# A two-layer graph convolution on one Trainium2 core: the order of its preparation, its PSUM banks and the row targets are rearranged

## The chip, the cores and the metric

The kernel runs on one core of a Trainium2 chip. The metric is the device time of one execution in microseconds. A core has five engines with an instruction queue each: PE (TensorE: matmuls and transposes), DVE (VectorE), ACT (ScalarE), POOL (GpSimd) and SP (SyncE, which only issues transfers). PE writes to PSUM, from where DVE or ACT copy the values to the on-chip memory. The engines wait for each other through semaphores.

## What is computed

The graph has N = 6250 nodes with 128 features each and E = 106250 edges, sorted by their target node. An edge has 64 message features and a time; the 32 cosines of the time difference to its source node are put ahead of the message. Two convolutions follow each other, and the sum with x is normalised:

```python
def _transformer_conv(h, edge_attr, src, dst, Wq, bq, Wk, bk, Wv, bv, We, Ws, bs):
    q = (h @ Wq + bq).reshape(n, H, C)                  # H = 2 heads of C = 64
    k = (h @ Wk + bk).reshape(n, H, C)
    v = (h @ Wv + bv).reshape(n, H, C)
    e = (edge_attr @ We).reshape(-1, H, C)
    kj = k[src] + e
    alpha = jnp.einsum('ehc,ehc->eh', q[dst], kj) / jnp.sqrt(C)
    a = <softmax of alpha over the edges of one target>
    out = segment_sum((v[src] + e) * a[:, :, None], dst, n)
    return out.reshape(n, H * C) + h @ Ws + bs

rel_t_enc = jnp.cos((last_update[src] - t)[:, None] * time_w + time_b)
edge_attr = jnp.concatenate([rel_t_enc, msg], axis=-1)
h = _transformer_conv(x, edge_attr, src, dst, ...)       # weights 1
h = relu((h - mean(h)) / sqrt(var(h) + 1e-5) * bn_g + bn_b)
h = _transformer_conv(h, edge_attr, src, dst, ...)       # weights 2
out = layernorm(x + h)
```

## The kernel before

The edges are cut into 104 chunks of 1024 (eight tiles of 128 edges, one edge per partition), and the nodes so that a chunk belongs to a window of 64 target nodes. Instead of keys and values per edge, the weights are multiplied together beforehand, and a table per target node (`tables`, L629) holds what its edges' raw features are multiplied with; a chunk's scores are then matmuls of its transposed rows with the table of its window.

**The rows of the source nodes** come by indirect transfers on POOL: one gather of 128 rows per tile, eight per chunk. In the first convolution they read `xv_d`, a copy of x with the node's time beside each row (L900), in the second h. The gathers write to a ring of seven slots in on-chip memory. Those of chunks 0 and 1 are made before `xv_d` exists: they read x (L1610), and their times are picked out of a table of hours by matmuls (`pick_times`, L670). A gather is issued four rounds ahead of its use. From chunk 7 on, when a slot is used again, it is tied to instructions of PE: the first gather of chunk k + 4, issued in round k, to the last matmul of round k − 1's sums (L1063).

**Rounds.** Round k of a convolution (L1150 and after) has the scores of chunk k (L1016), the divisions of chunk k − 2 (`divide`, L1072 to L1096), the lowest score per edge (L1024, DVE), the exponentials (L1031, ACT), the transposes of chunk k + 1 (L973, L985), the encoding of a later chunk's times (L938 to L946 on DVE, the sine L952 on ACT) and the sums of chunk k − 1 (L1063). At one place in a round, work from outside of the chunks is pulled (`rest`, L1389): in the first rounds two pieces each, at first the row targets (`targets`, L762), which say to which target row a chunk's boundary belongs, and then the tables of the other nodes, 512 nodes at a time. The order of a round's instructions on each engine is as written.

**The preparation** (`tile_gnn_resnorm`, L1484) comes ahead of both convolutions. Its steps are written as generators, each of which stops after one piece, and `step` calls put the pieces in an order. They are: the loads; columns of sources, targets and times from rows (`columns`, L1592 and after, transposes of PE and copies of DVE); the first gathers (L1610); the boundaries of the windows by a scan (L1646); the plan check, which gathers doubts about the input in `edge` and sets `oki` (L1696); the copy `xv_d` (`pass_features`, L526); the transposed x (`turn_features`, L650: four transposes of PE into PSUM, one copy of ACT, thirteen times); the products of the weights (`matrices`, L580); the picked times; and the tables of the first 512 nodes. When it is through, each engine reads `oki` (L1723) and branches to `ordered` (L712), which holds the convolutions, or to a general program that is not run here. POOL's next instructions after the branch are the gathers from chunk 2 on.

**PSUM in the preparation.** Four kinds of buffers: `fpt`, three tiles that are cut into twelve slices of 128 columns, each used once (`bank`, for weight products and codes); `fpx`, two buffers (`wide`, for columns, x0 and tables); `ftm`, two (`aside`, for the picked times and the boundaries); and `fxp`, a single one, for the transposes of x (`turning`).

**Queues.** Transfers are issued by SP and ACT (and the indirect ones by POOL). ACT's queue starts with rows of sources and targets, the weights of the first convolution (L1541), the column bs1 (L556) and two small pieces of the target rows, the tail (L1545); behind these stands ACT's first copy (L660).

Of the kernel before, what the change touches and what calls it, by code (L numbers as in the profile page):

```python
# [7 lines left out]
F32 = mybir.dt.float32  # L8
# [60 lines left out]
SQRT = 3  # L69
SWITCH = NC - 3  # L70
# [440 lines left out]
def load_features(nc, pl, x, node_vec):  # L511
# [6 lines left out]
    nc.sync.dma_start(pl.times, node_vec[:NF * P].rearrange("(p b) -> p b", b=NF))  # L518
    for i, (b0, b1) in enumerate(pl.cuts):
        nc.sync.dma_start(rows[:, b0:b1, 1:], x[:NF * P, :].rearrange("(p b) d -> p b d", b=NF)[:, b0:b1])  # L520
        if i == 0:
            nc.sync.dma_start(pl.rest[:NR, 1:], x[NF * P:N, :])
            nc.sync.dma_start(pl.rest[:NR, 0:1], node_vec[NF * P:N].rearrange("(p a) -> p a", a=1))

# [150 lines left out]
def pick_times(nc, pl, pool, bank, srows, node_vec):  # L675
# [16 lines left out]
    for k in range(EARLY):  # L692
        times = split_rows(pl, k)[2]
        for u in range(T // 4):
            pb = bank()
            nc.tensor.matmul(pb[:NA], one[:, k], hi[:, u * GE:(u + 1) * GE], start=True, stop=True)
            oh = pool.tile([NA, GE], F32, name="foh", bufs=2)
            nc.vector.tensor_scalar(oh, pb[:NA], lane[:NA], None, op0=OP.is_equal)
            yield
            pc = bank().rearrange("p (i n) -> p i n", n=P)  # L700
            for i in range(4):
                nc.tensor.matmul(pc[:, i], oh[:, i * P:(i + 1) * P], pl.hours, start=True, stop=True)
            for i in range(4):
                t = u * 4 + i
                junk = pool.tile([P, P], F32, name="fjunk", bufs=2)
                nc.vector.scalar_tensor_tensor(junk, pl.place_of, lo[:, t, k:k + 1], pc[:, i], op0=OP.is_equal,
                                               op1=OP.mult, accum_out=times[:, t, 0:1])
            yield
# [3 lines left out]
def ordered(ctx: ExitStack, tc: tile.TileContext, pl, x, dst, edge_attr_64, conv2, bn_g, bn_b, out):  # L712
# [49 lines left out]
    def targets():  # L762
# [11 lines left out]
        for i in range(NQ):  # L774
            nc.vector.tensor_sub(away[:, 0, i], nbq[:, :, i], nbq[:, :, 0])
# [4 lines left out]
        for q in range(NQ):  # L780
            nc.vector.tensor_sub(away[:, 2, q], past[:, NQ - 1], past[:, q])
# [29 lines left out]
    def conv(c, extra, first_blocks=None):  # L811
# [339 lines left out]
        with cs, tc.manual_schedule():  # L1151
            if c == 0:
                nc.vector.tensor_copy(rate, tw)
                nc.vector.tensor_copy(phase, tb)
            ended = None
# [179 lines left out]
    with tc.tile_pool(name="fpw", bufs=2) as pw:  # L1335
# [52 lines left out]
        def rest():  # L1388
# [5 lines left out]
            yield from targets()  # L1394
            yield
            for b0 in range(1, NT):
                yield from tables(nc, pl, 0, xT[:, b0 * GE:(b0 + 1) * GE], b0, pw, lambda: pl.bank())
# [93 lines left out]
def tile_gnn_resnorm(ctx: ExitStack, tc: tile.TileContext, x, src, dst, edge_attr_64, edge_weight, node_vec,  # L1491
# [11 lines left out]
    with tc.tile_pool(name="plan", bufs=1) as pl, tc.tile_pool(name="planw", bufs=2) as mw, \  # L1503
# [33 lines left out]
        nc.sync.dma_start(got.hours[:N // P], node_vec[:N // P * P].rearrange("(a b) -> a b", b=P))  # L1537
        nc.sync.dma_start(got.hours[N // P:, :N % P], node_vec[N // P * P:].rearrange("(a b) -> a b", a=1))
# [3 lines left out]
        got.bs1 = load_column(nc.scalar, keep, "fbs1", conv1["bs"])  # L1542
# [32 lines left out]
        def bank():  # L1575
            return next(fresh)
# [183 lines left out]
```

## Time and profile before

| | us |
|---|---|
| median of 3 runs (2184.24 to 2189.97) | 2184.45 |
| profiled execution | 2188.76 |
| its span | 2187.0 |
| PE busy (share of the span) | 1667.6 (76%) |
| POOL busy | 1578.8 (72%) |
| DVE busy | 1113.2 (51%) |
| ACT busy | 979.0 (45%) |

The mean granted clock of PE is 0.878 of full speed. A row of the time line has the start, the duration, the engine, the line of the kernel, the operation, output and input tiles (numbers of buffers left out), how many instructions it stands for, and in brackets the idle time of that engine before it and what released it. PEld is the weight load of PE, "ACTq" and the like are an engine's issuing of transfers. A releaser is worked out from semaphore events: the one that came last by the profile. Where an engine first loads `oki` and branches, as POOL does ahead of its first gather from `xv_d`, the branch itself is not shown.

### The profile page before, as it was taken

How to read it: one execution, taken by the hardware profiler on the slowest of the kernel's cores; microseconds unless marked ns; L12 is line 12 of the kernel's file. 1: busy time of each engine (PE TensorE's matmuls, PEld its weight loads, DVE VectorE, ACT ScalarE, POOL GpSimd, SP SyncE). 2: the span in 40 equal slices, each digit the busy share in tenths (PEclk: the TensorE clock that was granted, in tenths of full speed). 3: DMA queues.
4: the chain of work that ended last, by engine and by line, in shares of the span. 5: the costliest groups of instructions: out<-in, count | busy, mean ns of one | idle time of the engine just before them, and what ended most of it. 6: DMA issues, size and time to landing. Idle time of an engine off the chain costs nothing.

```text
span 2187.0 us, 45360 instructions
## 1 busy us (share of the span) xinstructions
PE 1667.6 (76%) x13293; PEld 981.9 (45%) x13293; DVE 1113.2 (51%) x3740; ACT 979.0 (45%) x1837; POOL 1578.8 (72%) x1686
## 2 busy tenths in 40 slices
PE   5798778767877787787767877777777877877776
PEld 3455455545454455455534433433444433443333
DVE  3676766656665766676737432333333332332233
ACT  2477666655544555576642333333332333232222
POOL 4567777777777777777637777777777777777774
PEclk9699999988988998999888887888988898888888
DMA  6578777776776777778758666676666667677662
GB/s 186 139 217 228 225 219 216 214 211 168 215 211 199 221 212 204 215 216 218 196 159 253 184 180 185 185 198 182 185 191 184 186 189 194 179 193 186 173 159 77
DMA packets 426908, 423.82 MB, mean 194 GB/s; under 512 B 297322, under 2 KB 344324, under 8 KB 423324
## 3 DMA queue, kind: packets, MB, share of 16 engines
q1 hardware_dynamic: 353344, 273.20, 43.8%
q0 software_dynamic: 53184, 109.44, 21.2%
q10 hardware_dynamic: 20124, 38.19, 4.8%
q8 instruction: 109, 1.79, 0.4%
q14 instruction: 147, 1.20, 0.2%
HBM read 274.75 MB, written 142.54 MB: 191 GB/s over the span
## 4 chain that ended last, share of the span: by engine, by line
PE 36%; DMA 33%; DVE 13%; issue 8%; POOL 4%; ACT 3%; SPq 1%; DVEq 0%; ACTq 0%; POOLq 0%
DMA fring<-hn_d,fsrcs 18%; PE fpa L1063 9%; DMA fring<-xv_d,fsrcs 8%; PE fps L1016 8%; PE fpx L973 5%; POOL fring L900 4%; PE fpg L634 3%; DMA et_d<-fet 3%; DVE farg L945 3%; PE fpe L985 2%; PE fpa L1094 2%; PE fppt L1040 1%; DVE fa L1075 1%; ACT L1031 1%; DVE farg L939 1%
## 5 line engine op out<-in xcount | busy, mean ns | idle before, releaser
L900 POOL DMA_INDIRECT fring<-xv_d,fsrcs x815 | 770.4, 945 | 287.5 <-issue 108.2
L900 POOL DMA_INDIRECT fring<-hn_d,fsrcs x775 | 734.5, 948 | 236.2 <-issue 106.7
L973 PE MATMUL fpx<-fident,fring 128*128 128x128 f32 x1664 | 326.9, 306 | 232.1 <-DMA fring<-hn_d,fsrcs 208.8
L1063 PE MATMUL fpa<-fring,fpt 128*32 128x256 f32 (+1 forms) x4128 | 407.7, 448 | 0.0
L977 ACT COPY fft<-fpx 128x512 f32<-128x512 f32 x402 | 233.5, 581 | 342.0 <-PE fpx L973 339.3
L973 PEld LDWEIGHTS fpx<-fident,fring 128*128 128x128 f32 x1664 | 223.8, 153 | 294.1 <-DMA fring<-hn_d,fsrcs 247.2
L1016 PE MATMUL fps<-fft,ftab 128*32 128x384 f32 (+1 forms) x1774 | 267.3, 526 | 69.5 <-ACT fs L1031 62.7
L1041 ACT COPY fpt<-fppt 128x384 f32<-128x384 f32 x208 | 100.0, 481 | 488.7 <-PE fppt L1040 462.6
L1063 PEld LDWEIGHTS fpa<-fring,fpt 128*32 128x32 f32 (+1 forms) x4128 | 141.6, 128 | 267.5 <-issue 175.9
L1144 DVE TENSOR_SCALAR fout<-fres,fmean,fvar 64x128 f32<-64x128 f32 x104 | 37.8, 364 | 339.9 <-ACT fvar L1142 328.0
L1094 PE MATMUL fpa<-fsel,fa 128*128 128x128 f32 x404 | 86.2, 297 | 142.3 <-DVE fsel L1079 134.0
L1024 DVE TENSOR_REDUCE flow<-fps 128x1 f32<-128x384 f32 x207 | 114.9, 555 | 111.0 <-PE fps L1016 109.8
L986 ACT COPY fet<-fpe 112x512 f32<-112x512 f32 x207 | 123.1, 595 | 83.8 <-DMA et_d<-fet 60.0
L985 PE MATMUL fpe<-fident,fring 128*112 128x128 f32 x832 | 145.3, 304 | 5.5 <-ACT fring L952 5.5
L1016 PE MATMUL fps<-fet,ftab 112*32 112x384 f32 (+2 forms) x960 | 145.5, 470 | 0.0
L1016 PEld LDWEIGHTS fps<-fft,ftab 128*32 128x32 f32 x1774 | 85.2, 118 | 133.4 <-ACT fs L1031 81.7
L945 DVE SCALAR_TENSOR_TENSOR farg<-fangles,farg 128x256 f32<-128x256 f32 x312 | 132.3, 424 | 10.7
L938 DVE TENSOR_TENSOR frel<-fring,few 128x8 f32<-128x8 f32 x104 | 18.2, 175 | 216.0 <-DMA fring<-xv_d,fsrcs 215.1
L1040 PE MATMUL fppt<-fident,fs 128*128 128x128 f32 x626 | 111.2, 287 | 18.2 <-DVE fhr L1354 7.4
L1031 ACT ACTIVATE fs<-fps,fm 128x384 f32<-128x384 f32 x207 | 120.5, 582 | 8.9 <-DVE fm L1026 7.9
L1094 PEld LDWEIGHTS fpa<-fsel,fa 128*128 128x128 f32 x404 | 48.7, 147 | 159.7 <-DVE fsel L1079 151.1
L1016 PE MATMUL fps<-fxT,ftab 112*32 112x384 f32 (+2 forms) x900 | 119.4, 497 | 1.1 <-DMA fxT<-et_d 1.1
(278 smaller groups left out, 2501.1 us busy)
## 6 DMA issues: line engine op xcount, KB each, us to landing
ea_d<-fring SPq DMA_DIRECT2D x104, 448.0 KB
et_d<-fet SPq DMA_DIRECT2D x104, 448.0 KB
fring<-ea_d SPq DMA_DIRECT2D x104, 448.0 KB
fxT<-et_d SPq DMA_DIRECT2D x104, 448.0 KB
tab_d<-fo ACTq DMA_DIRECT2D x26, 1024.0 KB
ftab<-tab_d SPq DMA_DIRECT2D x832, 32.0 KB
fring<-in_edge_attr SPq DMA_DIRECT2D x103, 256.0 KB
fring<-xv_d,fsrcs POOLq DMA_INDIRECT x815
```

Of the source, the lines that this page charges most:

```text
L900: row = nc.gpsimd.indirect_dma_start(out=f[:, t, :D + 1 - c], out_offset=None, in_=(h_d[:N, :] if k < RAW else hn_d) if c else pl.xv_d, in ...
L945: nc.vector.scalar_tensor_tensor(arg, turn, -part, arg, op0=OP.mult, op1=OP.add)
L973: last = nc.tensor.transpose(px[:, t * P:(t + 1) * P], s.x[:, u * 4 + t, 1 - c:1 - c + D], ident)
L977: nc.scalar.copy(s.ft[:, u * GE:(u + 1) * GE], px)
L985: last = nc.tensor.transpose(pe[:EC, t * P:(t + 1) * P], s.e[:, u * 4 + t], ident)
L986: copy(s.et[:, u * GE:(u + 1) * GE], pe[:EC])
L1016: steps.append(nc.tensor.matmul(s.ps[r, to:to + n], s.tab[:kd, r, i], (ets if i else fts)[:kd, at:at + n], start=i == 0, stop=i == 1 and t ...
L1024: nc.vector.tensor_reduce(low, s.ps, AX.X, OP.min)
L1031: nc.scalar.activation(s.s[:, :s.ps.shape[1]], s.ps, AF.Exp, bias=s.bias, scale=-1.0)
L1040: last = nc.tensor.transpose(pp[:, t * P:(t + 1) * P], s.s[:, t * P:(t + 1) * P], ident)
L1063: steps.append(nc.tensor.matmul(s.pa[g * GH:(g + of) * GH].rearrange("p (a d) -> p a d", a=2), s.pt[:, (g * n + t) * GH:(g * n + t + of) * ...
L1094: step = nc.tensor.transpose(s.po[:, i], s.a[:, r], s.sel[:, 0])
```

## The change

**PSUM.** The preparation has two kinds of buffers: `fpx`, four banks in turn for all its steps, `bank` being a slice of the next one; and `ftm`, four for the picked times. The single `fxp` and the one-time slices are gone.

**Picked times.** `pick_times` is cut differently. Its pieces are, chunk by chunk: `place` (two matmuls that spread a row of indices over the partitions), `find` (two comparisons), `pick` (eight matmuls); and at last `keep` for both chunks (DVE). Before, a piece was place and find, or pick and keep, of half a chunk.

**Order.** The `step` calls are placed anew. The first chunk's places, finds and picks stand ahead of the boundaries, the second's pick, the products of the weights from the keys' on, and x0 stand behind the plan check.

**Queues.** The hours go from SP to ACT, ahead of the weights; the column bs1 from ACT to SP, behind the times of the edges; the two tails from ACT to POOL, ahead of the iota for the identity; the times beside x go behind the first cut of x. On ACT a one-element copy (`warm`) stands behind the last issue.

**First convolution.** ACT loads the table of the sine by an instruction of its own at the start. The row targets' two loops of four subtractions are one subtraction each, and `targets` is pulled in two parts: the first in round 0, as before, the second in round 1 behind the first piece of the next table.

```diff
@@ load_features
-    nc.sync.dma_start(pl.times, node_vec[:NF * P]...)
     for i, (b0, b1) in enumerate(pl.cuts):
         nc.sync.dma_start(rows[:, b0:b1, 1:], ...)
         if i == 0:
...
+            nc.sync.dma_start(pl.times, node_vec[:NF * P]...)
@@ pick_times
+    def place(k):
+        for u in halves:
+            spread[u] = bank()
+            nc.tensor.matmul(spread[u][:NA], one[:, k], hi[:, u * GE:(u + 1) * GE], start=True, stop=True)
...
+    for act, k in ((place, 0), (find, 0), (pick, 0), (place, 1), (find, 1), (pick, 1), (keep, 0), (keep, 1)):
+        act(k)
+        yield
@@ targets
-        for i in range(NQ):
-            nc.vector.tensor_sub(away[:, 0, i], nbq[:, :, i], nbq[:, :, 0])
+        nc.vector.tensor_sub(away[:, 0], nbq.rearrange("a c i -> a i c"), nbq[:, None, :, 0].to_broadcast([1, NQ, NC]))
...
-        for q in range(NQ):
-            nc.vector.tensor_sub(away[:, 2, q], past[:, NQ - 1], past[:, q])
+        nc.vector.tensor_sub(away[:, 2], past[:, NQ - 1:].to_broadcast([1, NQ, NC]), past)
@@ conv
             if c == 0:
...
+                nc.scalar.add_instruction(mybir.InstLoadActFuncSet(..., act_func_set_id=TRIG))
@@ rest
-            yield from targets()
+            place = targets()
+            next(place)
             yield
             for b0 in range(1, NT):
-                yield from tables(nc, pl, 0, ..., b0, pw, lambda: pl.bank())
+                for i, _ in enumerate(tables(nc, pl, 0, ..., b0, pw, lambda: pl.bank())):
+                    yield
+                    if b0 == 1 and i == 0:
+                        next(place, None)
+                        yield
@@ tile_gnn_resnorm
-        nc.sync.dma_start(got.hours[:N // P], ...)
-        nc.sync.dma_start(got.hours[N // P:, :N % P], ...)
+        nc.scalar.dma_start(got.hours[:N // P], ...)
+        nc.scalar.dma_start(got.hours[N // P:, :N % P], ...)
...
-        got.bs1 = load_column(nc.scalar, keep, "fbs1", conv1["bs"])
+        warm = pl.tile([1, 2], F32, name="warm")
+        nc.gpsimd.memset(warm, 0.0)
+        nc.scalar.copy(warm[:, 0:1], warm[:, 1:2])
         tail = pl.tile([1, 2, NQ], I32, name="tail")
         for i, at in enumerate((-3 * P - 1, P)):
-            nc.scalar.dma_start(tail[:, i, :NQ - i], ...)
+            nc.gpsimd.dma_start(tail[:, i, :NQ - i], ...)
...
         rows(nc.sync, erows, edge_weight, CE)
+        got.bs1 = load_column(nc.sync, keep, "fbs1", conv1["bs"])
...
+        def wide():
+            return pp.tile([P, GE], F32, name="fpx", bufs=4)
         def bank():
-            return next(fresh)
-        def wide():
-            return pp.tile([P, GE], F32, name="fpx")
+            return wide()[:, :P]
         def aside():
-            return pp.tile([P, GE], F32, name="ftm")
-        def turning():
-            return pp.tile([P, GE], F32, name="fxp", bufs=1)
+            return pp.tile([P, GE], F32, name="ftm", bufs=4)
```

PE's queue in the preparation, before (L659 are the transposes of x, L696 the places, L702 the picks, L585 the transposes of weights, L600 and L604 their products):

```order
L659 MATMUL fxp<-fident,fhT 128x128 x8
L696 MATMUL ftm<-fhif,fone 49x512
L659 MATMUL fxp<-fident,fhT 128x128 x4
L585 MATMUL fpt_162<-fident,fwq_107 128x128
L585 MATMUL fpt_162<-fident,fwk_108 128x128
L702 MATMUL ftm<-fhours,foh 128x128 x4
L659 MATMUL fxp<-fident,fhT 128x128 x8
L696 MATMUL ftm<-fhif,fone 49x512
L585 MATMUL fpt_162<-fident,fwe_109 128x128
L659 MATMUL fxp<-fident,fhT 128x128 x4
L600 MATMUL fpt_163<-ftr_286,ftr_283 128x128
L604 MATMUL fpt_163<-fbq_111,ftr_286 128x1
```

And after (L660, L699, L710, L586, L601 and L605 are the same steps, L1703 is the plan check's matmul):

```order
L710 MATMUL ftm<-fhours,foh 128x128 x8
L660 MATMUL fpx<-fident,fhT 128x128 x4
L699 MATMUL ftm<-fhif,fone 49x512 x2
L660 MATMUL fpx<-fident,fhT 128x128 x8
L586 MATMUL fpx<-fident,fwq_107 128x128
L586 MATMUL fpx<-fident,fwk_108 128x128
L660 MATMUL fpx<-fident,fhT 128x128 x4
L1703 MATMUL fpx<-pones,worst 1x1
L586 MATMUL fpx<-fident,fwe_109 128x128
L660 MATMUL fpx<-fident,fhT 128x128 x4
L601 MATMUL fpx<-ftr_307,ftr_303 128x128
L605 MATMUL fpx<-fbq_111,ftr_307 128x1
```

All of them now take the next of the four banks `fpx`, the picks apart; the first chunk's picks have moved ahead of the first transposes of x, and the plan check's matmul ahead of the products of the weights.

DVE's queue in the first rounds, before, from the row targets' second part to the lowest score of chunk 1 (L1024):

```order
L788 TENSOR_SCALAR ftarget<-fpg,fhr 128x104
L792 SCALAR_TENSOR_TENSOR fhr<-fhr,ftarget 128x3
L793 SCALAR_TENSOR_TENSOR fhr<-fpg,fhr 128x3
L795 TENSOR_SCALAR fclosing<-fhr 128x2 x2
L796 TENSOR_SCALAR fhr<-fpg,fhr 128x104
L797 TENSOR_TENSOR fhr<-fhr,ftarget 128x104
L798 TENSOR_TENSOR fhr<-fhr 128x104
L799 TENSOR_TENSOR ftarget<-ftarget,fhr 128x104
L888 TENSOR_TENSOR fbits<-fdsts,fbitm 128x64
L890 TENSOR_SCALAR fring<-fbits 128x8x8
L891 TENSOR_SCALAR fring<-fbits 128x8x8
L1024 TENSOR_REDUCE flow<-fps 128x1
```

And after, from the lowest score of chunk 1 (now L1037) on (L951 to L959 are the encoding, L800 and after the targets' second part):

```order
L1037 TENSOR_REDUCE flow<-fps 128x1
L1039 TENSOR_SCALAR fm<-flow 128x1
L951 TENSOR_TENSOR frel<-fring,few 128x8
L952 TENSOR_TENSOR farg<-frel,fangles 128x256
L953 TENSOR_TENSOR farg<-farg,fangles 128x256
L955 TENSOR_SCALAR fangles<-farg 128x256
L956 TENSOR_SCALAR fangles<-fangles 128x256
L958 SCALAR_TENSOR_TENSOR farg<-fangles,farg 128x256 x3
L959 TENSOR_SCALAR farg<-farg 128x256
L800 TENSOR_SCALAR fhr<-fpg,fhr 128x104
L801 TENSOR_SCALAR ftarget<-fpg,fhr 128x104
L805 SCALAR_TENSOR_TENSOR fhr<-fhr,ftarget 128x3
```

The targets' second part has moved from ahead of that score to behind the encoding that follows it. On PE the scores of chunk 1 stood behind the target matmuls:

```order
L985 MATMUL fpe<-fident,fring 112x128 x4
L786 MATMUL fpg<-faway,pones 32x104 x12
L790 MATMUL fpg<-nbf,pones 128x3
L1016 MATMUL fps<-fft,ftab 32x384 x2
L1016 MATMUL fps<-fet,ftab 32x384 x2
```

After, these matmuls (L799, L803) come a round later, and a piece of the next table (L635) stands ahead of the scores (L1029):

```order
L998 MATMUL fpe<-fident,fring 112x128 x4
L635 MATMUL fpg<-fxT,fm_365 128x512
L1029 MATMUL fps<-fft,ftab 32x384 x2
L1029 MATMUL fps<-fet,ftab 32x384 x2
L1029 MATMUL fps<-fft,ftab 32x384 x2
L1029 MATMUL fps<-fet,ftab 32x384 x2
L1053 MATMUL fppt<-fident,fs 128x128 x3
L986 MATMUL fpx<-fident,fring 128x128 x4
L998 MATMUL fpe<-fident,fring 112x128 x4
L986 MATMUL fpx<-fident,fring 128x128 x4
L998 MATMUL fpe<-fident,fring 112x128 x4
L799 MATMUL fpg<-faway,pones 32x104 x12
```

What moved is the whole of the targets' share of PE, by one round of transposes and one of scores.

96 lines of the change are left out of this document (50 added, 46 removed).

## The prediction

> **What bounds the kernel now.** I read the page's groups first, then POOL's busy time by stage, then the time line of the places where POOL stops, and from there the waits.
>
> The page's group of the row gathers of the first convolution (busy time, mean ns, idle before):
>
> ```profile
> span 2187.0 us, 45360 instructions
> ...
> L900 POOL DMA_INDIRECT fring<-xv_d,fsrcs x815 | 770.4, 945 | 287.5 <-issue 108.2
> ```
>
> POOL's busy time by stretch (stretch, length, busy and count, granted clock, DMA share, GB/s):
>
> ```profile
> 45.00:95.00 50.00, 37.82 (x40) 0.72 0.48 117
> 95.00:116.00 21.00, 0.15 (x1) 0.77 0.58 170
> 116.00:600.00 484.00, 365.58 (x387) 0.93 0.77 213
> 600.00:1085.00 485.00, 366.04 (x388) 0.91 0.77 213
> 1085.00:1119.00 34.00, 0.83 (x1) 0.94 0.33 99
> 1119.00:2162.00 1043.00, 789.23 (x831) 0.84 0.68 187
> ```
>
> From 116 to 1085 us there are 387 and 388 gathers in 484 and 485 us: one each 484 / 387 = 1.25 us, and the first 40 stand just as densely (50 / 40 = 1.25). So POOL's gathers are one unbroken stream with two holes, 95 to 116 and 1085 to 1119. The second is the batch normalisation's, which the change doesn't touch. The first belongs to the start. The time line of POOL and PE there:
>
> ```profile
> 45.29 0.94 POOL L900 DMA_INDIRECT fring<-xv_d,fsrcs  x1 [17.42 <-DVE fb L606]
> ...
> 94.17 0.98 POOL L900 DMA_INDIRECT fring<-xv_d,fsrcs  x1 [0.30 <-issue]
> ...
> 106.77 1.50 PE L1063 MATMUL fpa<-fring,fpt 128*32 128x256 f32 x24
> ...
> 114.33 1.65 PE L1063 MATMUL fpa<-fring,fpt 128*64 128x256 f32 x20
> ...
> 116.28 0.94 POOL L900 DMA_INDIRECT fring<-xv_d,fsrcs  x1 [21.14 <-PE fpa L1063]
> ```
>
> Gather 41 belongs to chunk 7 and is tied to the sums of chunk 1 (L1063, ending at 114.33 + 1.65 = 115.98). From there on nothing but POOL's own pace is on the path up to 1085. Whatever moves the resume at 116.28 therefore moves the end by as much, and the question is only how much earlier the sums of chunk 1 come. Before them lie the preparation, up to 75.3, and three rounds, 75.3 to 116.
>
> **A: the preparation, four banks.** Its last steps on PE, ACT and DVE:
>
> ```profile
> 74.49 0.48 PE L664 MATMUL fxp<-fident,fxrest 128*128 128x128 f32 x1 [1.10 <-ACT fxT L660]
> 75.01 0.25 ACT L665 COPY fxT<-fxp 128x106 f32<-128x106 f32 x1 [0.57 <-PE fxp L664]
> 75.29 0.20 DVE L1153 COPY fangles<-ftw 128x32 f32<-128x32 f32 x1 [1.13 <-ACT fxT L665]
> ```
>
> The turning of x ends the stage, and the first encoding waits for it (in the changed order too). The waits up to 76 us that belong to it (total, times, longest):
>
> ```profile
> ACT L660 <- DMA tail<-in_dst: 21.2, 1, 21.2
> ACT fxT L660 <- PE fxp L659: 20.0, 10, 2.8
> PEld fxp L659 <- ACT fxT L660: 12.1, 4, 7.4
> ```
>
> The time line where the longest begins:
>
> ```profile
> 19.28 0.34 ACTq L556 DMA_DIRECT2D fbs<-in_L_gnn_bs  x1
> 19.66 1.47 ACTq L1545 DMA_DIRECT2D tail<-in_dst  x2
> 21.17 1.28 ACT L660 ACT_TABLE_LOAD   x1 [21.17 <-DMA tail<-in_dst]
> ...
> 23.52 0.72 PEld L659 LDWEIGHTS fxp<-fident,fhT 128*128 128x128 f32 x4 [7.38 <-ACT fxT L660]
> ```
>
> ACT can't copy until its last issues are through at 21.17, and PE, with one buffer fxp, stands 7.38 us behind the copy; three further waits of the same kind make 12.1 us. With four banks PE can be several groups ahead of ACT, and without the bs1 column and the tails ACT's queue ends with the weight loads. I take the whole 12.1 off the stage's end: PE is the engine that must get through its list. The lower bound is the one long wait, 7.4, if the three short ones come back as waits for data. The upper bound comes from PE's busy time (same columns as above):
>
> ```profile
> 6.00:60.00 54.00, 35.04 (x127) 1.00 0.66 188
> 60.00:70.00 10.00, 10.00 (x26) 0.51 0.46 128
> 70.00:75.00 5.00, 3.87 (x15) 0.50 0.27 57
> ```
>
> PE works 35.04 + 10.00 + 3.87 = 48.9 of 69 us, so at unchanged durations at most 69 − 48.9 = 20.1 can go. Moving the later weight products, x0 and the second chunk's times behind the plan check changes the order in which PE does this work, not its amount: 0 for the stage's end. The plan check itself comes earlier, and with it POOL's first gather (45.29); that only lengthens POOL's hole, unless the resume comes before the fortieth gather's end at 95.2, that is with a gain over 21 us.
>
> The row 60 to 70 also bears on a rule of the Trainium skill: by TensorE: Matmul & The Clock Gate, Part 1, some 3.4 us of sustained work open the gate to full clock. Here PE is busy for the whole 10 us at a granted 0.51, so the trace disagrees; Part 4 of that page, by which transposes in transpose mode don't count as such work, fits it better. By the first rule the denser PE would go to full speed and the gain would be that of the second rival; by the row it stays as it is.
>
> **A': the queues.** The tail's two issues go to POOL, ahead of the iota on which the identity hangs. PE's first transposes also need srows:
>
> ```profile
> 5.14 0.69 DVE L1594 CAST rowf<-srows 104x1024 f32<-104x1024 int32 x1 [1.13 <-DMA srows<-in_src]
> ```
>
> DVE still waited 1.13 us for that transfer after it had made the identity, so this much of a delay is hidden. No plain DMA issue on POOL is in the trace. From below the price is nothing (two issues of 1.47 / 2 = 0.74 us as on ACT's queue, 1.5, nearly covered by 1.13); from above two indirect gathers at 1.25, 2.5. I take 0.5 lost: nearer to the plain issues, which are of the same kind. fhours on ACT, its times load later and bs1 on SP cost issues of some 0.3 us on queues that are through long before the values are used: 0, covered by the wait for x.
>
> The Trainium skill's DMA: Bandwidth & Descriptors, in its table at the top, puts the first byte of a DMA from GpSimd at about 1 us and from SP or ACT at about 0.6, which speaks against this move; two such issues would lose an estimated 0.8 by it. No run here shows it.
>
> **B: the sine's table.** The first round's sine:
>
> ```profile
> 79.60 0.53 DVE L946 TENSOR_SCALAR farg<-farg 128x256 f32<-128x256 f32 x1
> ...
> 80.19 1.28 ACT L952 ACT_TABLE_LOAD   x1 [4.94 <-DVE farg L946]
> 81.49 0.51 ACT L952 ACTIVATE fring<-farg,qpi 128x256 f32<-128x256 f32 x1
> ```
>
> ACT idles 4.94 us ahead of the load. Ordered before the sine's operand is ready, its 1.28 us lie in this gap: 1.3 gained, since PE waits for the sine. If the cover were gone, 0.
>
> **C: row targets in two parts.** The first two rounds, DVE, ACT and PE:
>
> ```profile
> 91.54 0.60 ACT L986 COPY fet<-fpe 112x512 f32<-112x512 f32 x1
> ...
> 93.74 1.08 DVE L775 TENSOR_TENSOR faway<-nbf 1x104 f32<-1x104 f32 x4
> ...
> 96.65 0.78 DVE L781 TENSOR_TENSOR faway<-fpast 1x104 f32<-1x104 f32 x4
> ...
> 98.07 0.33 DVE L787 TENSOR_SCALAR fhr<-fpg,fhr 128x104 f32<-128x104 f32 x1 [0.64 <-PE fpg L786]
> 98.48 1.52 PE L1016 MATMUL fps<-fft,ftab 128*32 128x384 f32 x8
> ...
> 100.23 0.27 DVE L799 TENSOR_TENSOR ftarget<-ftarget,fhr 128x104 f32<-128x104 f32 x1
> ...
> 101.37 0.56 DVE L1024 TENSOR_REDUCE flow<-fps 128x1 f32<-128x384 f32 x1 [0.40 <-PE fps L1016]
> ...
> 108.34 0.16 DVE L1072 TENSOR_SCALAR finv<-fpa 128x1 f32<-128x1 f32 x1 [1.76 <-PE fpa L1063]
> ```
>
> PE's scores of chunk 1 (98.48) stand behind the target matmuls, which wait for DVE's faway; their operands were there at 91.54 + 0.60 = 92.14. In the new order nothing of the targets stands ahead of them. DVE's minimum of these scores (101.37) stands behind the second part, 98.07 to 100.50 = 2.4 us and its wait of 0.64, which now stands a round later, and the two groups of four small operations (1.08 + 0.78 = 1.86) become one operation each; at most they keep 0.78 + 0.78, at least 2 × 0.27 (a fourth of the first). The minimum so comes up to 2.4 + 0.64 + 1.3 = 4.4 us earlier. But the 2.4 us are not gone: they stand now behind the next encoding and ahead of the division of chunk 0 (108.34), which also has to wait for PE's targets and one table step. Only the operations saved (0.3 to 1.3), the wait of 0.64 and part of DVE's and PE's idle time ahead of 108.34 (1.76) are a net gain for it: 0.3 at least, 1.3 + 0.64 + 1.76 = 3.7 at most. I take 2.5, nearer to the upper end, because both waits named are for matmuls that this order issues earlier.
>
> **The sum.** 12.1 − 0.5 + 1.3 + 2.5 = 15.4 us earlier. The profiled execution took 2188.76 us (span 2187.0): 2173.4 by its own time. It lies 4.3 us over the median of the three runs, 2184.45; the shift is one of the start and holds for each, so 2184.45 − 15.4 = 2169.0.
>
> **The rivals.** *The banks free little* (chance 0.2). The row of 20.0 us shows ACT waiting for PE ten times, so past the first long wait neither engine holds the other for long, and PE may meet waits for x or for the picked times instead; with the cover of A' gone as well: 7.4 − 2.5 + 1.3 + 0.3 = 6.5, and 2178.0. This is the case of a change that mostly does not do what it says. Against it speaks that three of the four waits of PE still make 12.1 − 7.4 = 4.7.
>
> *All of PE's gaps go, or its clock rises* (0.17): 20.1 − 0.5 + 1.3 + 3.7 = 24.6. At this point POOL's own first forty gathers become the bound if they don't start earlier, at 21: so 21 to 24.6, at about 22.8 and 2161.7. For it speaks that 0.51 in 60 to 70 leaves room; against it, that PE's work depends on x's arrival, on DVE for the picked times and on ACT for the weight products.
>
> *Cold rounds* (0.04, slower). The clock of PE in the first rounds:
>
> ```profile
> 94.00:104.00 10.00, 8.83 (x55) 0.52 0.72 212
> 104.00:112.00 8.00, 8.00 (x71) 0.96 0.54 156
> ```
>
> A round at full clock takes 114.33 − 106.77 = 7.6 us; at 0.52 it would take 7.6 × 0.96 / 0.52 = 14.0, where POOL needs 8 × 1.25 = 10. Were PE to stay at half clock past the resume, each round would lose 4.0; it decides from (15.4 + 6.6) / 4.0, that is from six rounds on, and eight would give 2184.45 − 15.4 + 32 = 2201. Against it: the clock came back at 104 after one round of dense work. For it, the Trainium skill's clock gate page, "A second HAM failure mode": cycling through PSUM banks leaves PE small gaps in which it falls back to half clock; no run here shows it so far.
>
> **The numbers.** What a measurement of this kernel can tell from no change is about 0.3%, 6.6 us: faster is below 2177.9, slower above 2191.0. My forecast has 0.59: 2169.0; with A at 12.1 and the bounds of A' and C it has 12.1 − 2.5 + 1.3 + 0.3 = 11.2 to 12.1 + 1.3 + 3.7 = 17.1, that is 2167.3 to 2173.3. The first rival lies on the edge of faster, half of it within 0.3%. Faster 0.59 + 0.17 + 0.10 = 0.86, same 0.10, slower 0.04. The range leaves out the slow case, part of the second rival and the far side of the first: 2161 to 2178.
>
> **What would show it.** In the changed kernel's trace: the first encoding's copy (75.29) near 63.5; no wait of PE for a copy of fxT above a microsecond; ACT's first copy ahead of 19; PE's row in the last ten microseconds of the preparation still at about 0.5; the table load in a gap of ACT; scores of chunk 1 within 17 us of the first encoding (98.48 − 75.29 = 23.2 now); POOL's resume near 101 in place of 116.28, and its gathers 1.25 us apart from there to the hole of the normalisation, itself 33 to 34 us as before. Wrong if the resume moves by less than 7 or more than 21, or if it moves and the end doesn't follow: then POOL's stream is not the path that I take it for.

## The result, and the profile after

The changed kernel takes 2169.1 us (median of four runs, 2168.36 to 2170.15), the kernel before beside it 2184.34; the ratio is 0.9924, with a 95% interval of 0.9907 to 0.9942. That is 15.2 us less, and by the interval 12.7 to 20.3. The profiled execution took 2170.15 us (span 2168.3); against the profiled execution of before, whose span was 2187.0, it is 18.7 us shorter. The rest of this document reads the two traces, so its shifts are some 3.5 us larger than that of the medians.

In all sets of the experiments but the last one's the kernel before itself took 2656 to 2694 us, its engines standing still for nothing that the profile shows, from about 58 us on (47 with the buffers alone; ACT of the changed kernels from about 20), so these sets are read by their ratios, by stretches that lie ahead of that, and, against runs of the same level, by PE's busy time.

**The resume.** POOL's time line in the changed kernel, its first gather from `xv_d`, the resume, the first convolution's last gather, and the second's first and last:

```profile
36.15 0.95 POOL L913 DMA_INDIRECT fring<-xv_d,fsrcs  x1 [2.28 <-DVE foh L704]
...
96.50 0.94 POOL L913 DMA_INDIRECT fring<-xv_d,fsrcs  x1 [10.16 <-PE fpa L1076]
...
1065.46 0.95 POOL L913 DMA_INDIRECT fring<-xv_d,fsrcs  x1 [0.30 <-PE fpx L986]
1098.80 0.94 POOL L913 DMA_INDIRECT fring<-h_d,fsrcs  x1 [32.39 <-DMA h_d<-fhr]
...
2143.50 0.95 POOL L913 DMA_INDIRECT fring<-hn_d,fsrcs  x1 [0.30 <-issue]
```

The resume moved from 116.28 to 96.50, by 19.8 us, the last gather of the first convolution from 1084.88 to 1065.46, by 19.4, and the first of the second from 1119.09 to 1098.80, by 20.3. So the start reaches the batch normalisation one to one. In the second convolution 2.5 us are given back (2161.31 to 2143.50 is 17.8).

**The preparation's end.** PE, ACT and DVE where the first round begins:

```profile
56.81 0.42 PE L665 MATMUL fpx<-fident,fxrest 128*128 128x128 f32 x1
...
57.92 0.28 ACT L666 COPY fxT<-fpx 128x106 f32<-128x106 f32 x1
58.22 1.28 ACT L1168 ACT_TABLE_LOAD   x1
58.24 0.20 DVE L1166 COPY fangles<-ftw 128x32 f32<-128x32 f32 x1 [3.87 <-DMA ftab<-tab_d]
...
62.93 0.51 ACT L965 ACTIVATE fring<-farg,qpi 128x256 f32<-128x256 f32 x1 [3.42 <-issue]
```

The first encoding starts at 58.24 in place of 75.29, 17.1 us earlier. It starts right behind ACT's copy at 57.92, as before, whatever the releaser's name says. The table load lies in ACT's gap: from the first encoding to the end of the sine it was 82.00 − 75.29 = 6.71 us, and is 63.44 − 58.24 = 5.20.

**PE in the preparation.** The stretch from 5 us to the first encoding, of the changed kernel (length, busy and count, granted clock):

```profile
5.00:58.20 53.20, 40.69 (x165) 0.87 0.76 215
```

and of the kernel before:

```profile
5.00:75.30 70.30, 49.02 (x165) 0.89 0.60 171
```

The same 165 instructions take 40.69 us in place of 49.02. Two things shorten them: the clock, and how closely they follow each other. First the clock. The changed kernel's picks of chunk 0, and its transposes of x, four to a group:

```profile
21.95 3.78 PE L710 MATMUL ftm<-fhours,foh 49*128 49x128 f32 x16
...
25.66 1.11 PE L660 MATMUL fpx<-fident,fhT 128*128 128x128 f32 x4
...
33.81 0.60 PE L660 MATMUL fpx<-fident,fhT 128*128 128x128 f32 x4
...
38.18 1.11 PE L660 MATMUL fpx<-fident,fhT 128*128 128x128 f32 x4
...
47.36 0.60 PE L660 MATMUL fpx<-fident,fhT 128*128 128x128 f32 x4
...
53.59 3.42 PE L660 MATMUL fpx<-fident,fhT 128*128 128x128 f32 x16 [1.43 <-DVE few L1617]
```

A group that stands alone costs 0.60 at full clock and 1.11 at half. Before, all but one were at 1.06 to 1.12; now three are at 0.60. The last sixteen take 3.42 / 4 = 0.86 each while the granted clock is 0.50: they gain by following each other without a gap. The stretches of granted full and half clock of the changed kernel, from the first record of the clock on:

```profile
33.43:36.84 3.41, 2.89 (x27) 1.00 0.47 111
36.84:47.08 10.24, 9.25 (x36) 0.50 0.37 78
47.08:53.91 6.83, 5.20 (x26) 1.00 0.47 160
53.91:57.32 3.41, 3.32 (x17) 0.50 0.77 237
```

and of the kernel before:

```profile
53.38:60.20 6.82, 5.77 (x27) 1.00 0.44 142
60.20:75.30 15.10, 13.67 (x39) 0.50 0.39 102
```

Ahead of these the column says 1.00, but the transposes take the time of half clock in both kernels. So PE is busy at full clock for 2.89 + 5.20 = 8.1 us in place of 5.8. At 0.60 against 1.11 these 2.3 us more are worth about 2 of the 8.3 us (an estimate); the other 6 are the same instructions closer together.

**The start.** DVE's first copy of the source rows and PE's first work in the changed kernel:

```profile
9.71 0.69 DVE L1611 CAST rowf<-srows 104x1024 f32<-104x1024 int32 x1 [4.28 <-DMA srows<-in_src]
...
10.46 1.65 PE L1616 MATMUL fpx<-fident,rowf 104*128 104x104 f32 x8 [10.46 <-DVE rowf L1611]
```

Both come 4.6 us later than before (5.14 and 5.89). DVE waits for the source rows' transfer. SP's queue in the changed kernel:

```profile
0.74 0.40 SPq L1549 DMA_DIRECT2D srows<-in_src  x1
1.20 0.43 SPq L520 DMA_DIRECT2D fhT<-in_x  x1
```

The first cut of x is now issued at 1.20, while ACT still issues the other parts of the source rows (from 0.75, the last at 2.91, as it did); in the kernel before it stood at 2.87, behind three small loads. From 2 to 6 us the DMA engines move 269 GB/s in the changed kernel and 189 before.

### The profile page after: what moved, and what is told of

Read it like the earlier page. It is cut to its first block, busy times and chain, and to the rows that moved or that the text cites. A ratio compares the mean times of both kernels' runs of the same rounds, so it can differ in the third digit from the quotient of the medians.

```text
span 2168.3 us, 45360 instructions
## 1 busy us (share of the span) xinstructions
PE 1674.1 (77%) x13293; PEld 990.9 (46%) x13293; DVE 1115.7 (51%) x3734; ACT 977.9 (45%) x1838; POOL 1586.6 (73%) x1689
## 4 chain that ended last, share of the span: by engine, by line
PE 22%; DMA 20%; issue 4%; POOL 3%; DVE 1%; ACT 0%; POOLq 0%; DVEq 0%; ACTq 0%
DMA fring<-hn_d,fsrcs 19%; PE fpa L1076 8%; PE fps L1029 4%; POOL fring L913 3%; PE fpg L635 3%; PE fpx L986 2%; DMA fring<-h_d,fsrcs 1%; PE fppt L1053 1%; PE fpa L1121 1%; PE fpg L1464 1%; PE fpa L1122 1%; PE fpa L1107 0%; DMA out<-fout 0%; PE fpg L1366 0%; PE fpg L1076 0%
## 5 line engine op out<-in xcount | busy, mean ns | idle before, releaser
L986 PE MATMUL fpx<-fident,fring 128*128 128x128 f32 x1664 | 334.2, 311 | 230.9 <-DMA fring<-hn_d,fsrcs 216.2
L986 PEld LDWEIGHTS fpx<-fident,fring 128*128 128x128 f32 x1664 | 228.8, 156 | 294.9 <-DMA fring<-hn_d,fsrcs 255.0
L1029 PE MATMUL fps<-fft,ftab 128*32 128x384 f32 (+1 forms) x1774 | 269.4, 524 | 70.5 <-ACT fs L1044 63.9
L1037 DVE TENSOR_REDUCE flow<-fps 128x1 f32<-128x384 f32 x207 | 114.9, 555 | 115.0 <-PE fps L1029 112.7
L1029 PE MATMUL fps<-fet,ftab 112*32 112x384 f32 (+2 forms) x960 | 147.9, 471 | 0.0
L1029 PEld LDWEIGHTS fps<-fft,ftab 128*32 128x32 f32 x1774 | 85.8, 118 | 134.1 <-ACT fs L1044 81.6
L951 DVE TENSOR_TENSOR frel<-fring,few 128x8 f32<-128x8 f32 x104 | 18.1, 174 | 206.4 <-DMA fring<-xv_d,fsrcs 184.9
L1029 PE MATMUL fps<-fxT,ftab 112*32 112x384 f32 (+2 forms) x900 | 121.0, 500 | 1.6 <-DMA fxT<-et_d 1.6
L998 PEld LDWEIGHTS fpe<-fident,fring 128*112 128x112 f32 x832 | 115.1, 153 | 6.8 <-ACT fring L965 5.3
```

What stands on the lines that cost most here:

```text
L986: last = nc.tensor.transpose(px[:, t * P:(t + 1) * P], s.x[:, u * 4 + t, 1 - c:1 - c + D], ident)
L998: last = nc.tensor.transpose(pe[:EC, t * P:(t + 1) * P], s.e[:, u * 4 + t], ident)
L1029: steps.append(nc.tensor.matmul(s.ps[r, to:to + n], s.tab[:kd, r, i], (ets if i else fts)[:kd, at:at + n], start=i == 0, stop=i == 1 and t ...
L1037: nc.vector.tensor_reduce(low, s.ps, AX.X, OP.min)
```

## The experiments

All are compared with the kernel before in their own set.

### The kernel before, once more

> The kernel before, unchanged, for a second profile. If the two profiles show the preparation as it is on every execution: first encoding at 75 us, POOL's resume at 116 us, within 1 us, and PE at about half clock in its last 15 us. If PE's clock in the preparation differs between executions: a resume 3 to 5 us earlier, which would be the reason why the profiled execution lay 4 us above the median. Time 2184 to 2190.

Measured: 2659.26 us beside 2656.49, ratio 1.0008 (0.9994 to 1.0021). Its first 48 us repeat the first profile: the target rows' copy at 48.36 (48.45 there), the first gather at 45.20 (45.29), PE's busy time in the preparation 49.12 (49.02). So PE's slow preparation belongs to the kernel and not to one execution. The stall of the engines begins behind that, so the run doesn't say why the first profiled execution lay 4 us above its median; this stays open.

### The buffers alone

```diff
-        small = [... three tiles "fpt" ...]
         def bank():
-            return next(fresh)
+            return wide()[:, :P]
         def wide():
-            return pp.tile([P, GE], F32, name="fpx")
+            return pp.tile([P, GE], F32, name="fpx", bufs=4)
         def aside():
-            return pp.tile([P, GE], F32, name="ftm")
+            return pp.tile([P, GE], F32, name="ftm", bufs=4)
-        def turning(): ...
...
-    turned = turn_features(nc, got, turning, N)
+    turned = turn_features(nc, got, wide, N)
```

> The kernel before with only the PSUM buffers of the change: four banks in turn for all steps, four for the picked times, order, queues and row targets as before. Theory (buffers and order each give a part): PE's three short waits for ACT's copies go (4.7 us), the long one shrinks only as far as four banks reach while ACT is held until 21 us; resume near 110, time 2177 to 2181. Rival (the buffers are the whole effect): 12 us at least, resume at 104 or before, 2172 or less. Rival (the order is the whole effect): under 2 us, 2183 or more.

> The kernel before with only the buffers of the change, once more, in a set whose kernel before takes 2184 us. Theory (a part each): resume near 110, 2177 to 2181. Rival (buffers are the whole effect): resume at 104 or before, 2172 or less. Rival (order is the whole effect): 2183 or more.

Measured: 2650.24 beside 2656.49, ratio 0.9975 (0.9963 to 0.9987), and 2685.49 beside 2692.41, 0.9979 (0.9966 to 0.9993). The times in the expectations don't apply to such a set, but the order of PE's work is that of before, so the undisturbed part can be compared step by step. DVE's copy of the target rows in the kernel before of this set:

```profile
48.36 0.79 DVE L1594 CAST rowf<-drows 104x1024 f32<-104x1024 int32 x1
```

and with the buffers alone:

```profile
15.60 1.97 PE L659 MATMUL fpx<-fident,fhT 128*128 128x128 f32 x8
...
21.60 1.28 ACT L660 ACT_TABLE_LOAD   x1 [21.60 <-issue]
...
38.67 0.81 DVE L1588 CAST rowf<-drows 104x1024 f32<-104x1024 int32 x1
```

The same step comes 9.7 us earlier (39.07 in the second set, 9.3 before the same 48.36). That lies between the 6 us of the theory and the 12 of the rival, at a step ahead of the preparation's end. PE turns two groups at once at 15.60 and goes on, while ACT is still held to 21.60 by its queue: of the long wait, 7.0 us of PE's idle time in the first profile, 3.3 are left (5.5 in the second set). PE's busy time up to the first encoding falls from 49.12 to 43.16 and 42.94, with the very same instructions. How, a product of the weights shows, in the kernel before of this set and then with the buffers alone, both at half clock by the groups of transposes beside them (1.11 and 1.12):

```profile
44.93 0.79 PE L600 MATMUL fpt<-ftr,ftr 64*128 64x128 f32 x2 [0.25 <-DVE fb L606]
```

```profile
35.75 0.80 PE L600 MATMUL fpx<-ftr,ftr 64*128 64x128 f32 x4
```

Two that stand alone take as long as four in a row. The clock gives the smaller part: at granted full clock PE is busy for 7.25 us (42.92 to 53.16) in place of 5.42 (52.81 to 59.64). So the buffers remove waits and let PE's work run closer together. What they give behind this step, and what the new order gives beside them, isn't shown: the engines' standing still lies in between.

### A single buffer in the changed kernel

```diff
         def wide():
-            return pp.tile([P, GE], F32, name="fpx", bufs=4)
+            return pp.tile([P, GE], F32, name="fpx", bufs=3)
+        def turning():
+            return pp.tile([P, GE], F32, name="fxp", bufs=1)
-    turned = turn_features(nc, got, wide, N)
+    turned = turn_features(nc, got, turning, N)
```

> The changed kernel with the transposes of x in a single PSUM buffer of their own again (three banks are left for the other steps). Theory: PE waits for ACT's copy between every two groups again, above all in the last sixteen transposes that stand in a row; resume 4 to 8 us later than 96.5, time 2174 to 2178. Rival (order and PE's clock are the effect): within 1.5 us of the changed kernel, 2168 to 2170.5.

> The changed kernel with a single buffer for the transposes of x, once more, in a set whose kernel before takes 2184 us. Theory (PE waits for each copy again): resume 4 to 8 us after 96.5, 2174 to 2178. Rival (order and PE's clock are the effect): within 1.5 us, 2168 to 2170.5.

Measured: 2657.4 beside 2656.49, ratio 1.0002 (0.9994 to 1.0011), and 2690.77 beside 2692.41, 1.0004 (0.9989 to 1.0018). The waits of the first of these up to its first encoding at 109.94:

```profile
PEld fxp L660 <- ACT fxT L661: 24.5, 8, 9.2
PE fxp L660 <- ACT fxT L661: 19.0, 8, 7.6
```

PE waits for a copy eight times, where the control (below, the changed kernel in a set of the same level) has one such wait, of 0.7 us. The sum is an upper bound, since ACT's own standing still is in the longest of them. Free of it are the waits between the last transposes:

```profile
102.50 1.12 PE L660 MATMUL fxp<-fident,fhT 128*128 128x128 f32 x4 [1.10 <-ACT fxT L661]
104.72 1.11 PE L660 MATMUL fxp<-fident,fhT 128*128 128x128 f32 x4 [1.10 <-ACT fxT L661]
106.93 1.12 PE L660 MATMUL fxp<-fident,fhT 128*128 128x128 f32 x4 [1.10 <-ACT fxT L661]
```

The groups stand 2.2 us apart, where the changed kernel took 3.42 us for all sixteen transposes (53.59, above). PE's busy time up to the first encoding is 49.15 and 51.28, against 45.54 in that control, although order and queues are the change's. The run with the targets whole (below) has the changed kernel's preparation in the second of these sets: its first encoding is at 103.08 where the single buffer's is at 113.44, its busy time 47.18, its time 2683.78 against 2690.77. All that the change gains in such a set is lost, and the rival (order and clock without the buffers) falls for such a set. No run shows the single buffer without the engines' standing still, which it passes on to PE, so its price there stays open.

### The loads as before

```diff
-        nc.scalar.dma_start(got.hours...)
+        nc.sync.dma_start(got.hours...)
@@ load_features
+    nc.sync.dma_start(pl.times, ...)
     for i, (b0, b1) in enumerate(pl.cuts):
...
-            nc.sync.dma_start(pl.times, ...)
```

> The changed kernel with the hours back on SP and the node times ahead of the first cut of x, as before; the tails stay on POOL. In the changed kernel the source rows reach DVE at 9.7 us in place of 5.1. Theory (x's first cut, issued 1.7 us earlier, takes the bandwidth from the source rows): the rows are there near 5.2, PE starts near 6, and the start's 4.6 us reach the resume: near 92, time 2164 to 2166. Rival (the tails on POOL delay the rows): PE starts at 10 still, 2169. Rival (x's arrival bounds the preparation, not its start): PE starts at 6, but the resume stays within 1.5 us of 96.5, 2168 to 2170.

> The changed kernel with the hours back on SP and the node times ahead of the first cut of x, once more, in a set of runs whose kernel before takes its 2184 us. Theory (the source rows are there at 5.3 in place of 9.7, and the start's 4.4 us reach the resume): resume near 92, time 2164 to 2166. Rival (x's arrival bounds the preparation): resume within 1.5 us of 96.5, 2168 to 2170.

> The changed kernel, unchanged, beside the kernel before on the same chip, as the control for the sets above. If this set's kernel before takes 2184 us: ratio 0.9907 to 0.9942 as at first, resume near 96.5. If it takes 2650 to 2690 as in the two sets before (engines standing without anything that the profile shows): theory (the part up to 58 us is undisturbed, so the start is won as before, and POOL isn't the bound later): source rows at DVE at 9.5, first gather from xv_d near 36, ratio 0.997 to 0.999, between one bank (1.000) and the loads as before (0.995). Rival (the order of the loads is not the reason of that 0.995): ratio at 0.995 or 0.996 as well.

> The changed kernel with the hours on SP and the node times ahead of x, beside the control in one set. Theory: source rows 4 us earlier, the preparation's undisturbed part 4 us earlier throughout, time 3 to 6 us under the control's. Rival (x's arrival bounds): the rows earlier, the first gather and the time within 1.5 us of the control's.

> The changed kernel with the hours on SP and the node times ahead of x, a last time. If the set's kernel before takes 2184 us and POOL is the bound: theory (the start's 4.4 us reach the end), resume near 92 and 2164 to 2166; rival (x's arrival bounds), resume within 1.5 us of 96.5 and 2168 to 2170. If it takes 2650 or more: ratio 0.994 to 0.996, as in the sets before.

Measured: 2646.96, 2678.82, 2643.0 and 2680.27 us; ratios 0.996 (0.9946 to 0.9974), 0.995 (0.9934 to 0.9967), 0.995 (0.9929 to 0.9972) and 0.9938 (0.9916 to 0.996). The control, the changed kernel, had 2645.57 beside 2657.46, 0.9955 (0.9941 to 0.9968). The control was expected at a ratio of 0.997 to 0.999 and came out where its rival had it. By the whole time control and experiment can't be told apart in their common set: 2643.0 and 2645.57, with intervals that overlap, where 3 to 6 us had been expected. By the trace they can. The control's source rows:

```profile
10.17 0.69 DVE L1611 CAST rowf<-srows 104x1024 f32<-104x1024 int32 x1 [4.72 <-DMA drows<-in_dst]
```

and with the loads as before:

```profile
5.35 0.72 DVE L1611 CAST rowf<-srows 104x1024 f32<-104x1024 int32 x1
```

All four runs have them at 5.35 to 5.43, with the tails still on POOL: it is the order of the loads, not the tails, that delays the source rows. That x's first cut takes the bandwidth from them is argued from the queues' rows; no run varied this cut alone. What comes behind moves along: the first gather from `xv_d` 42.15 to 37.41, the first encoding 102.11 to 98.49, the resume 140.09 to 136.17, all about 4 us earlier, as the theory had it.

### The row targets in one piece

```diff
-            place = targets()
-            next(place)
+            yield from targets()
             yield
             for b0 in range(1, NT):
-                for i, _ in enumerate(tables(...)):
-                    yield
-                    if b0 == 1 and i == 0:
-                        next(place, None)
-                        yield
+                yield from tables(...)
```

> The changed kernel with the row targets pulled in one piece again, their loops still one operation each. Theory (the split is worth most of term C, 2.5 less the operations saved): resume 1 to 2 us later, 2170 to 2171. Rival (the split is worth nothing, since its second part only stands elsewhere): within 0.5 us of 96.5, 2168.5 to 2169.7. Rival (the split saves the whole 4 us of the scores' wait): resume near 100.5, 2173.

Measured: 2683.78 beside 2692.41, ratio 0.9975 (0.9964 to 0.9986). The control stood in another set, so only the stretch from the sine to the resume is compared: with the targets whole it ends at 141.89 after a sine at 107.76, that is 34.1 us, in the control at 140.09 after 106.80, 33.3. The split so is worth about 0.8 us, but the runs with the loads as before, which have the split too, show 33.0 to 34.7 for the same stretch (136.17 − 103.17 = 33.0 in one, 137.89 − 103.16 = 34.7 in another). The size can't be told from nothing by these runs.

### All queues as before, with banks, order, table load and targets of the change

```diff
 (the loads as before, and)
-        got.bs1 = load_column(nc.sync, keep, "fbs1", conv1["bs"])
+        got.bs1 = load_column(nc.scalar, keep, "fbs1", conv1["bs"])
...
-            nc.gpsimd.dma_start(tail[:, i, :NQ - i], ...)
+            nc.scalar.dma_start(tail[:, i, :NQ - i], ...)
```

> The changed kernel with all loads in their old queues: hours on SP, node times ahead of x, bs1 and the tails on ACT behind the weights. Banks, order, the sine's table and the targets are the change's. Theory (the queue part of the change only costs, because four banks hide ACT's late start): source rows at 5.2, PE starts at 6, ratio as with the hours and times alone put back, 0.994 to 0.995. Rival (the tails on ACT hold its first copy at 21 us and PE with it): ACT's first copy behind 21 us while PE waits, ratio 0.996 to 0.998.

Measured: 2160.88 us (2160.59 to 2163.88) beside 2184.59, ratio 0.9892 (0.9874 to 0.9909). It is faster than both kernels, 8.2 us under the changed one's 2169.1; its kernel before agrees with that of the first set within 0.3 us. Its time line:

```profile
5.38 0.69 DVE L1611 CAST rowf<-srows 104x1024 f32<-104x1024 int32 x1 [1.12 <-DMA drows<-in_dst]
...
6.12 1.65 PE L1616 MATMUL fpx<-fident,rowf 104*128 104x104 f32 x8 [6.12 <-DVE rowf L1611]
...
17.62 3.78 PE L710 MATMUL ftm<-fhours,foh 49*128 49x128 f32 x16
...
21.10 1.28 ACT L1569 ACT_TABLE_LOAD   x1 [21.10 <-DMA tail<-in_dst]
...
21.33 1.11 PE L660 MATMUL fpx<-fident,fhT 128*128 128x128 f32 x4
22.37 3.64 PE L699 MATMUL ftm<-fhif,fone 2*49 2x512 f32 x4
22.49 1.00 ACT L661 COPY fxT<-fpx 128x512 f32<-128x512 f32 x1
...
54.61 0.20 DVE L1166 COPY fangles<-ftw 128x32 f32<-128x32 f32 x1 [3.91 <-ACT fxT L666]
...
93.01 0.94 POOL L913 DMA_INDIRECT fring<-xv_d,fsrcs  x1 [5.07 <-PE fpa L1076]
```

ACT is held by the tails until 21.10, just as before the change, and PE doesn't feel it: in the new order PE turns x for the first time at 21.33, after the first chunk's picked times, and has further banks. The rival falls, and the theory stands: the queue part of this change gains nothing that the buffers and the order don't give, and it costs the start. Source rows and PE's start are 4.3 us earlier than in the changed kernel, the first encoding 3.6, the resume 3.5 (93.01 against 96.50).

The rest of the 8.2 us lies far behind. The second convolution's first and last gather in this kernel:

```profile
1095.25 0.94 POOL L913 DMA_INDIRECT fring<-h_d,fsrcs  x1 [33.37 <-DMA h_d<-fhr]
...
2134.39 0.95 POOL L913 DMA_INDIRECT fring<-hn_d,fsrcs  x1 [0.30 <-issue]
```

At 1095.25 it is 3.6 us ahead of the changed kernel's 1098.80, at 2134.39 it is 9.1 ahead of 2143.50. The second convolution has the same instructions in both, and takes 1039.1 us here, 1044.7 there and 1042.2 before. No run here says why. Gathers that come more than 1.3 us after the one before, the latest of them in its first rounds, are late by 2.5 us in all here (beyond 1.25 us each), by 6.5 in the changed kernel and by 5.3 before, so they hold most of the difference. So 3.5 us of this kernel's lead are shown as the price of the queues, and the other 5 are only measured.

## Why the prediction was right, and where its sum was not

**What bounds the kernel: right.** The resume moved by 19.8 us, the end of the first convolution by 19.4; POOL's gathers stand 1.25 us apart as before.

**A, 12.1 us: the gaps were right, PE's own work and the start were not.** PE's idle time between its start and the first encoding was 75.29 − 5.89 less its busy 49.02, that is 20.4 us, and is 58.24 − 10.46 − 40.69 = 7.1: 13.3 less, close to the 12.1 that I took from the row of PE's waits. But I set the upper bound at unchanged durations, and wrote that the new order changes the order of PE's work, not its amount. Its busy time fell by 8.3, and gaps and busy time together by 21.6, more than the bound of 20.1. Some 6 of the 8.3 come because the same instructions run closer together: how long PE is busy depends on the spacing of its instructions too, which I had not seen. About 2 are the clock's, which is in the second rival, to which I had given 0.17. The reason against the clock was the row of ten busy microseconds at 0.51. What exactly lets the clock rise is not settled. The changed kernel's PE from 10 to 30 us, and its second half:

```profile
10.00:30.00 20.00, 16.61 (x53) 1.00 0.97 279
20.00:30.00 10.00, 10.00 (x36) 1.00 0.87 286
```

From 20 to 30 us it is busy without a break, and the transposes at 25.66 still take the 1.11 of half clock, so the Trainium skill's rule of some 3.4 us of sustained work (TensorE: Matmul & The Clock Gate, Part 1) isn't borne out by the row. Whether Part 4 of that page in the Trainium skill, by which transposes don't count as such work, explains it, these rows can't tell: transposes stand between the picks (21.95) and the next places here.

**A', 0.5 us: the wrong place and the wrong size.** I priced the tails on POOL and held the moved loads for free, "covered by the wait for x". The tails cost at most 0.3 (source rows at 5.35 to 5.43 with them on POOL, 5.14 before), and none of it is shown to be theirs, since the rows are at 5.38 with the tails on ACT too. The loads cost nearly all of the 4.6 at PE's start, most likely because the small loads on SP had kept the first cut of x behind the source rows. The step that failed is that one: I asked whether the moved values come in time, and not what takes their place in the queue. The Trainium skill's figure for transfers from GpSimd (DMA: Bandwidth & Descriptors, the table at the top) would have given an estimated 0.8 for the tails; the trace shows less, and the loss elsewhere.

**B, 1.3 us: right.** From the first encoding to the end of the sine it is 1.5 us less, the load's 1.28 and 0.2 beside it.

**C, 2.5 us: half of it.** From the sine's end to the resume it was 116.28 − 82.00 = 34.3 and is 96.50 − 63.44 = 33.1: 1.2. The rows of DVE and PE in the changed kernel show where the rest went:

```profile
72.01 1.00 PE L1029 MATMUL fps<-fft,ftab 128*32 128x384 f32 x6 [0.88 <-ACT fs L1044]
...
78.26 0.55 DVE L1037 TENSOR_REDUCE flow<-fps 128x1 f32<-128x384 f32 x1
...
83.99 2.07 PE L635 MATMUL fpg<-fxT,fm 128*128 128x512 f32 x2 [2.28 <-DVE fhr L806]
85.99 2.49 PE L1076 MATMUL fpa<-fring,fpt 128*32 128x256 f32 x24
...
88.56 0.16 DVE L1085 TENSOR_SCALAR finv<-fpa 128x1 f32<-128x1 f32 x1 [2.75 <-PE fpa L1076]
```

Counted from the first encoding, the scores of chunk 1 come at 72.01 − 58.24 = 13.8 us in place of 23.2, and their minimum at 20.0 in place of 26.1. But the division of chunk 0 comes at 30.3 in place of 33.1, and there DVE waits 2.75 us for the sums on PE, which take 2.49 us at half clock (granted 0.50 from 81.2 to 88.0) in place of 1.50. The sums stand behind a table step that has itself waited 2.28 us for the targets' second part on DVE (L806); the prediction named this wait and set no price on it. What the split gives early is given back there. The two groups of small operations take 0.90 and 0.58 us in place of 1.08 and 0.78, which saves 0.4, near the lower end of the 0.3 to 1.3.

**The sum.** At the resume 17.1 + 1.5 + 1.2 = 19.8 us, where the prediction had 11.6 + 1.3 + 2.5 = 15.4. That its time, 2169.0, met the median 2169.1 is partly chance: PE's shorter busy time (8.3 for it) and the delayed start (4.6 against it) were both unforeseen, and the shift of the medians is 3.5 us smaller than that of the two profiled spans, of which the one of before lay 4.3 above its median.

**The signs.** Those of the waits, the table load, the scores (13.8, within 17) and the gathers came as written, and the normalisation's hole is 32.4. Two didn't: ACT's first copy of x is at 26.81 and not ahead of 19, because in the new order it waits for PE (its one-element copy is at 19.35), and PE's clock in the preparation's last ten microseconds is 0.83 (48 to 58) and not about 0.5.

**The rivals.** "The banks free little" was wrong: at the target rows the buffers alone give 9.7 us. "All of PE's gaps go, or its clock rises" came about by half: 7.1 us of gaps are left, and POOL's first stream still ends 10.16 us before the resume. The cold rounds didn't come; but one sum of chunk 0 at half clock, above, is a small piece of that mechanism.

## What to carry to other kernels

A single buffer between a producer and a consumer can cost more than the waits that the profile books on it: when PE was no longer interrupted, the same matmuls also took less busy time, mostly because they followed each other closely, to a lesser part by the clock. A load that is moved out of a queue lets the next one go earlier, and that one may be the large transfer that now competes with what the first engine is waiting for; look at the first wait of the trace after each such move. And a change of several parts should be taken apart even when it gains: here its queue part cost some 3.5 of the microseconds that the rest had won.

## What was not expected of the hardware

The granted-clock column can't be relied on at the start: it says 1.00 from 10 to 30 us, where four transposes took 1.11 us, and 1.00 from 6 to 60 in the kernel before, where seven of eight such groups did; the durations of equal instructions tell the clock there. PE's busy time for the same 165 instructions lay between 40.7 and 51.3 us, with the waits between them; the clock is the smaller part of that where it could be told apart. The order of the loads at the start counts: the same source rows reached DVE at 5.1 to 5.4 us or at 9.4 to 10.2, by whether the loads ahead of x's first cut (768 KB by the profile's list of issues) let it go at 2.87 or at 1.20. That the cut takes the bandwidth from them is the likely reason and not shown alone.
